# One ring of twelve tiles in place of two rings of six for a selective scan

## The chip, the cores and the metric

The kernel runs on one core of one Trainium2 chip, as one program. The metric is the device time of that program in microseconds (us); lower is better. For a profiled execution the span from the first to the last instruction on the core is given too.

## What is computed

The reference is a network of four layers on four images of 96 channels and 64x64 pixels. Layer 0 is the one that the change touches. It normalises the image, projects each pixel to 192 inner channels, convolves, and then runs a selective scan over the 4,096 pixels in four directions k. In each direction there are 16 states for each of the 192 channels:

```python
def step(h, inp):
    d_t, u_t, b_t, c_t = inp
    dA = jnp.exp(d_t[..., None] * A)
    h = dA * h + (d_t * u_t)[..., None] * b_t[:, :, None, :]
    y = jnp.einsum('bkdn,bkn->bkd', h, c_t)
    return (h, y)
```

So a decay dA and an inflow are made for every pixel, channel and state, the recurrence h = dA * h + inflow runs along the pixels, and the sum over the states of h times c gives the output y. Layer 1 is a deformable convolution (with gathers), layer 2 a Fourier mixer and a quantised feed-forward block, layer 3 a linear attention and another such block.

## The kernel before

**Units.** The scan of layer 0 is cut into units of 128 rows (8 channels x 16 states) by 1,024 pixels (T). There are 4 images x 4 directions x 4 stretches of pixels x 24 groups of 8 channels = 1,536 units. `Layer0.scan` (L898) goes through them in a written-out order and issues, for iteration n, pieces of several units at once, each on its own engine:

- `fetch` of unit n+5 (L964): a DMA on ACT's queue (L993) spreads 8 rows of the step sizes `de` over 128 rows of a tile `da` (512 KB).
- `decay` of unit n+2 (L1011): ACT turns `da` into exp(da * A), in place (L1014).
- `inflow` of unit n+1 (L1016): two matmuls on PE (L1020) spread 8 rows of `du` over 128 rows of a PSUM tile `db`; there are two such tiles.
- `enter` of unit n+1 (L1029): DVE multiplies `db` by the B rows of the tile `bc`, in place (L1034).
- `recur` of unit n (L1036): DVE's scan instruction reads `da` and `db` and writes the states `hh` (L1042).
- `weigh` of unit n-2 (L1046): POOL copies the last state (L1049) and multiplies `hh` by the C rows of `bc`, in place (L1051).
- `total` of the pair n-5 and n-4, in odd iterations (L1053): PE sums the states with eight matmuls that read `hh` (L1070). The text calls this the fold. For the first pair of a block it starts with matmuls on the tile `ad` (L1065).
- `settle` and `store` (L1078, L1083): ACT copies eight units' sums out of PSUM (L1081), and SP writes them to memory.

**Rings.** The tile pool gives the tiles of one name in turn: `da` has six buffers (L991) and `hh` six (L1040), each of 4 KB per partition. An instruction that starts to fill a buffer waits for all users of the tile that had it before. So the fetch of unit n+5, six units behind, waits until the scan of unit n-1 has read its `da`; and the scan of unit n waits until the fold of unit n-6 has read its `hh`.

**Order of the work.** The order on each engine is fixed when the program is built; every engine works through its list in that order. `layers23` (L1859) interleaves the scan with two streams of side work (the preparation of later images, layers 1 to 3 of earlier images). A planner (`Clock`, L206) holds an expected end for each engine; a stream may add a step if the engines that the step needs are not too far ahead of the planner's time (`has_room`, L231). `recur` adds 2.33 us to DVE's expected end, not before the decay and the fold that frees its buffer are expected to be done (L1039; the fold's time is passed in at L949). No wait on the chip comes from the planner: only the order does.

Of the kernel before, what the change touches and what calls it, by code (L numbers as in the profile page):

```python
# [8 lines left out]
F32 = mybir.dt.float32  # L9
# [14 lines left out]
T = 1024  # L24
# [335 lines left out]
class Net:  # L360
# [29 lines left out]
    def load(self, name, pool, tag=None):  # L390
        src = self.ins[name]
        t = pool.tile(list(src.shape), F32, name="w_" + name, tag=tag or "w_" + name)
        self.nc.sync.dma_start(t, src)
        return t
# [160 lines left out]
class Layer0:  # L555
# [342 lines left out]
    def scan(self):  # L898


        units = [
            Unit(b, k, step, g, i, q)
            for b in range(B)
            for k in ((1, 3, 0, 2) if b else (0, 1, 3, 2))
            for step in range(NT)
            for g in range(NG)
            for i in range(4)
            for q in range(2)
        ]
        ahead = 5  # L910
        loaded = 0
        clock = self.net.clock

        def at(m):
            return units[m] if 0 <= m < len(units) else None

        def made(u):
            return all(
                (u.b, u.k, both, 2 * u.j + h) in self.ready for both in (False, True) for h in range(2)
            )  # L920

        for n in range(len(units) + 7):
            for m in range(loaded, min(n + ahead + 1, len(units))):
                while not made(units[m]):
                    yield False
            if n == 0:
                while loaded < ahead:
                    self.fetch(units[loaded], units[loaded - 1] if loaded else None)
                    loaded += 1
                self.decay(at(0))  # L930
                self.decay(at(1))
                self.inflow(at(0))
                self.next = at(0)
                self.enter()

            for period, tick, load in ((24, 12, self.fetch_step), (8, 2, self.fetch_block)):
                u = at(n - n % period + period)
                if n % period == tick and u is not None and made(u):
                    load(u)
            for stage, m in ((self.inflow, n + 1), (self.decay, n + 2)):  # L940
                if at(m) is not None:
                    stage(at(m))
            if n % 2 == 1 and at(n - 5) is not None:
                self.total(at(n - 5), at(n - 4))
            if loaded < len(units):
                self.fetch(units[loaded], units[loaded - 1])
                loaded += 1
            if at(n) is not None:
                self.recur(at(n), at(n - 6).summed if n >= 6 else 0.0)  # L949
            if at(n - 2) is not None:  # L950
                self.weigh(at(n - 2))
            if n % 2 == 0 and at(n - 6) is not None and at(n - 6).i == 3:
                self.settle(at(n - 6))
            if n % 2 == 1 and at(n - 7) is not None and at(n - 7).i == 3:
                self.store(at(n - 7))
            clock.unit(self.scanned[1])
            self.next = at(n + 1)
            if self.next is not None:
                clock.enter, clock.entered = self.enter, self.next.spread
            yield True  # L960
            if clock.enter:
                self.enter()

    def fetch(self, u, before):  # L964


        sp, nc = self.sp, self.net.nc
        b, k, j, g, ts = u.b, u.k, u.j, u.g, u.ts
        c0 = 64 * g
        halves = [slice(j * T + h * CH, j * T + (h + 1) * CH) for h in range(2)]  # L970
        if not u.first_of_step:
            u.bc = before.bc
        elif u.bc is None:
            self.fetch_step(u)
        if u.first_of_step and u.step == 0:
            u.state = sp.tile([128, DI // D8], F32, name=f"st{u.key}", tag="st")
        else:
            u.state = before.state
        if not u.first_of_block:
            u.du, u.sums = before.du, before.sums  # L980
        else:
            u.sums = {"add": None}
            if u.du is None:
                self.fetch_block(u)
        if u.i == 1 and u.s == 1 and (k == 0 or u.back):
            add = u.sums["add"] = sp.tile([128, CH], F32, name=f"ad{u.key}", tag="ad", bufs=1)
            src = self.y_d[b][k - 2] if u.back else self.u_d[b]
            for h in range(2):
                nc.scalar.dma_start(add[64 * h : 64 * h + 64], src[c0 : c0 + 64, halves[h]])
        self.net.clock.add(ACT, 0.6, self.scanned[1])  # L990
        u.da = sp.tile([128, T], F32, name=f"da{u.key}", tag="da", bufs=6)  # L991
        src = self.de_d[b][k][c0 + 32 * u.q + u.i : c0 + 32 * u.q + 32 : 4, ts]
        nc.scalar.dma_start(u.da, src.unsqueeze(0).to_broadcast([NS, D8, T]))  # L993

# [41 lines left out]
    def recur(self, u, free):  # L1036

        nc, clock = self.net.nc, self.net.clock
        self.scanned = (self.scanned[1], clock.add(DVE, 2.33, max(u.decayed, free)))  # L1039
        u.hh = self.sp.tile([128, T], F32, name=f"hh{u.key}", tag="hh", bufs=6)  # L1040
        first = 0.0 if u.step == 0 else u.state[:, u.n : u.n + 1]
        nc.vector.tensor_tensor_scan(  # L1042
            u.along(u.hh), u.along(u.da), u.along(u.db), first, ALU.mult, ALU.add
        )
# [896 lines left out]
```

## Time and profile before

| | us |
|---|---|
| median of three runs | 8518.56 |
| the three runs, lowest to highest | 8506.89 to 8540.53 |
| profiled execution | 8585.65 |
| its span | 8582.9 |
| first scan starts, last scan starts | 183.3, 7487.1 |

The profile page gives the busy time of each engine over the span, and groups of instructions by line; "idle before, releaser" is the time for which the engine stood before instructions of that group, and the work of another engine (or DMA) that ended most of it. PE is the matmul engine and PEld its weight loads, DVE the vector engine, ACT the scalar engine, POOL the GpSimd; ACTq marks what ACT's sequencer issues itself, DMAs among it. The views of waits list who waited for whom, with the total in us, the number of times and the longest one.

### The profile page before, as it was taken

What the parts mean: (1) busy time and instruction counts of PE and PEld (TensorE: products, weight loads), DVE (VectorE), ACT (ScalarE), POOL (GpSimd) and SP (SyncE); (2) the same over time, 40 slices, a digit from 0 to 9 for tenths busy, and PEclk for the clock granted to TensorE, in tenths of its full rate; (3) what the DMA queues carried; (4) which work ended last, traced back from release to release, by engine and by line L of the source; (5) the groups of instructions that cost most, each with busy time, mean ns of one, the idle gap of its engine ahead of it and who ended that gap; (6) DMA issues with size and microseconds to landing.
All of it is one profiled execution on the core that took longest, in us unless ns stands there. A gap on an engine that the chain in (4) does not pass through costs nothing.

```text
span 8582.9 us, 96776 instructions
## 1 busy us (share of the span) xinstructions
PE 6491.0 (76%) x31814; PEld 2822.5 (33%) x31848; DVE 6815.3 (79%) x5122; ACT 4923.9 (57%) x8979; POOL 5616.1 (65%) x4308
## 2 busy tenths in 40 slices
PE   6775877679767668777767889777788777887487
PEld 2211221122222223311223555214454332464274
DVE  2799889888799888688898888888888887727614
ACT  5664566546567767755566667554667774423124
POOL 1565567656579888666688887675788986517600
PEclk9766877679668779877777888778788877888698
DMA  3677678868789888876788989777898886734410
GB/s 97 168 198 193 167 196 221 212 159 204 189 215 249 224 228 222 202 190 187 205 229 225 235 227 228 172 174 188 223 243 219 210 212 168 176 103 131 131 56 20
DMA packets 773929, 1608.29 MB, mean 187 GB/s; under 512 B 264081, under 2 KB 355757, under 8 KB 771222
## 3 DMA queue, kind: packets, MB, share of 16 engines
q10 hardware_dynamic: 244224, 843.17, 38.4%
q1 hardware_dynamic: 455478, 532.37, 24.0%
q0 software_dynamic: 73728, 226.57, 9.9%
q8 instruction: 255, 4.18, 0.2%
q14 instruction: 244, 2.00, 0.1%
HBM read 1345.43 MB, written 256.29 MB: 187 GB/s over the span
## 4 chain that ended last, share of the span: by engine, by line
PE 35%; DVE 30%; DMA 9%; issue 9%; ACT 9%; POOL 4%; SPq 1%; ACTq 1%; another core or an unknown queue 1%; DVEq 0%; POOLq 0%
DVE hh L1042 15%; DVE db L1034 8%; PE pc L763 4%; PE py L1070 4%; PE ps L1416 3%; PE f L1510 3%; POOL hh L1051 3%; ACT g L1395 2%; PE pd L1432 2%; PE db L1020 2%; DMA da<-de 2%; ACT da L1014 2%; PE h L1551 1%; PE zp L1576 1%; DMA m<-in_dft 1%
## 5 line engine op out<-in xcount | busy, mean ns | idle before, releaser
L1051 POOL TENSOR_TENSOR hh<-hh,bc 128x1024 f32<-128x1024 f32 x1536 | 3670.2, 2391 | 348.3 <-DVE hh L1042 230.6
L1042 DVE TENSOR_TENSOR_SCAN hh<-da,st,db 128x1024 f32<-128x1024 f32 x1152 | 2701.3, 2345 | 205.3 <-PE py L1070 68.5
L1034 DVE TENSOR_TENSOR db<-db,bc 128x1024 f32<-128x1024 f32 x1536 | 1863.1, 1213 | 561.7 <-PE db L1020 542.2
L1014 ACT ACTIVATE da<-da,w_al 128x1024 f32<-128x1024 f32 x1536 | 1736.9, 1145 | 496.0 <-DMA da<-de 144.5
L1383 POOL DMA_INDIRECT g<-table,idx x1152 | 1190.6, 1034 | 410.9 <-issue 185.9
L1020 PE MATMUL db<-du,rep 24*128 24x512 bf16 x3072 | 697.7, 453 | 802.4 <-DVE hh L1042 752.2
L1070 PE MATMUL py<-hh,w_fold 128*32 128x512 f32 x6144 | 1115.9, 786 | 30.9 <-POOL hh L1051 18.0
L1395 ACT ACTIVATE g<-g,wt 128x96 f32<-128x96 f32 x3456 | 965.0, 364 | 133.5 <-PE py L1070 38.9
L1042 DVE TENSOR_TENSOR_SCAN hh<-da,db 128x1024 f32<-128x1024 f32 x384 | 877.1, 2284 | 73.9 <-PE py L1070 23.6
L1416 PE MATMUL ps<-w_ident,g 128*96 128x128 f32 x3744 | 690.5, 331 | 246.3 <-issue 122.2
L1020 PEld LDWEIGHTS <-rep 24*128 24x128 bf16 x3072 | 160.3, 93 | 1914.3 <-issue 1278.0
L851 POOL TENSOR_TENSOR lw<-lw,w 128x512 f32<-128x512 f32 x192 | 244.1, 1272 | 710.9 <-DVE w L849 668.5
L1416 PEld LDWEIGHTS ps<-w_ident,g 128*96 128x96 f32 x3744 | 501.6, 149 | 594.1 <-issue 211.2
L1049 POOL COPY st<-hh 128x1 f32<-128x1 f32 x1152 | 234.6, 204 | 648.4 <-DVE hh L1042 612.7
L763 PE MATMUL pc<-pad,wc 96*128 96x512 f32 x1152 | 570.8, 632 | 8.8 <-ACT st L1424 2.6
L1424 ACT COPY st<-ps 96x384 f32<-96x384 f32 x384 | 180.3, 472 | 578.9 <-PE ps L1416 421.5
L882 PE MATMUL pr<-ex,w_ident 128*128 128x512 f32 x384 | 299.7, 872 | 146.7 <-DVE ex L872 57.1
L840 PE MATMUL pd<-xd,w_dtw 103*64 103x512 f32 (+1 forms) x512 | 281.5, 818 | 71.2 <-DVE rl L853 26.9
L1432 PE MATMUL pd<-st,wdc 96*128 96x256 f32 x1152 | 323.0, 434 | 11.6 <-ACT st L1424 4.2
L763 PEld LDWEIGHTS pc<-pad,wc 96*128 96x128 f32 x1152 | 217.2, 199 | 311.8 <-issue 291.0
L1519 ACT COPY d<-f 128x512 f32<-128x512 f32 x192 | 111.3, 582 | 315.2 <-PE f L1510 282.3
L1070 PEld LDWEIGHTS py<-hh,w_fold 128*32 128x32 f32 x6144 | 160.9, 125 | 385.9 <-issue 293.3
(259 smaller groups left out, 8798.4 us busy)
## 6 DMA issues: line engine op xcount, KB each, us to landing
da<-de ACTq DMA_DIRECT2D x1536, 512.0 KB
du<-du SPq DMA_DIRECT2D x1536, 96.0 KB
bc<-bcd SPq DMA_DIRECT2D x128, 512.0 KB
y<-yb SPq DMA_DIRECT2D x384, 128.0 KB
de<-rl SPq DMA_DIRECT2D x128, 256.0 KB
m<-in_dft SPq DMA_DIRECT2D x128, 256.0 KB
ad<-y ACTq DMA_DIRECT2D x192, 128.0 KB
table<-pix SPq DMA_DIRECT2D x256, 96.0 KB
```

The costliest lines, as they stand in the source:

```text
L763: nc.tensor.matmul(pp, lhsT=wc[:, q, g * 128 : (g + 1) * 128], rhs=pad[:, r0 + dy : r0 + dy + NR, dx : dx + W], start=(q == 0), stop=(q == 8),
L882: nc.tensor.matmul(pr, lhsT=net.ident, rhs=ex, start=True, stop=False)
L1014: self.net.nc.scalar.activation(u.da, u.da, AF.Exp, scale=self.al[:, a : a + 1])
L1020: self.net.nc.tensor.matmul(db[:, h, :], lhsT=self.rep[64 * u.q + 32 * h : 64 * u.q + 32 * h + 24], rhs=u.du[64 * u.q + 32 * h : 64 * u.q ...
L1034: self.net.nc.vector.tensor_mul(u.db, u.db, u.bc[:, 0, :])
L1042: nc.vector.tensor_tensor_scan(u.along(u.hh), u.along(u.da), u.along(u.db), first, ALU.mult, ALU.add)
L1051: self.net.nc.gpsimd.tensor_mul(u.hh, u.hh, u.bc[:, 1, :])
L1070: nc.tensor.matmul(py[p0 : p0 + 32], lhsT=self.fold[:, u.i, :], rhs=hc[:, h * CH : (h + 1) * CH], start=u.sums["add"] is None and u.i == 0 ...
L1383: nc.gpsimd.indirect_dma_start(out=g[:, k, :], out_offset=None, in_=self.tables[b % 2], in_offset=bass.IndirectOffsetOnAxis(ap=idx[:, n : ...
L1395: nc.scalar.activation(pixel, pixel, AF.Identity, scale=wt[:, n, c : c + 1])
L1416: nc.tensor.matmul(pt[:, k, :], lhsT=g[:, k, c * C : (c + 1) * C], rhs=net.ident, is_transpose=True, start=(c == 0), stop=(c == corners - 1),)
L1432: nc.tensor.matmul(po, lhsT=wdc[:, k, :], rhs=st[:, k, :], start=(k == 0), stop=(k == 8))
```

## The change

The scan writes its states into the tile that holds the decay, so `hh` is `da`. The ring of `hh` is gone, and the ring of `da` gets its six buffers too. The planner's entry for the scan takes the fold of unit n-9 in place of that of unit n-6.

```diff
@@ def scan(self):
             if at(n) is not None:
-                self.recur(at(n), at(n - 6).summed if n >= 6 else 0.0)
+                self.recur(at(n), at(n - 9).summed if n >= 9 else 0.0)
@@ def fetch(self, u, before):
         self.net.clock.add(ACT, 0.6, self.scanned[1])
-        u.da = sp.tile([128, T], F32, name=f"da{u.key}", tag="da", bufs=6)
+        u.da = sp.tile([128, T], F32, name=f"da{u.key}", tag="da", bufs=12)
         src = self.de_d[b][k][c0 + 32 * u.q + u.i : c0 + 32 * u.q + 32 : 4, ts]
         nc.scalar.dma_start(u.da, src.unsqueeze(0).to_broadcast([NS, D8, T]))
@@ def recur(self, u, free):
         self.scanned = (self.scanned[1], clock.add(DVE, 2.33, max(u.decayed, free)))
-        u.hh = self.sp.tile([128, T], F32, name=f"hh{u.key}", tag="hh", bufs=6)
+        u.hh = u.da
```

With twelve buffers in one ring, the fetch of unit n+5 now gets the buffer of unit n-7, whose last user is the fold of unit n-7.

## The prediction

> **What bounds the kernel now.** I first read the busy times of the page and the busy times by stretch, to see which stage sets the time. From 183 to 7490 us the scan runs; after it 1,093 us of side work are left, which the change doesn't touch. In the listing of instructions per engine, built from both kernels, the number behind the last scan is the same on DVE (765) and POOL (314) and nearly so on PE (3,284 before, 3,256 after) and ACT (596, 595). So the scan's stretch decides.
>
> ```profile
> core 0: us, PE busy (x) PEld busy (x) DVE busy (x) ACT busy (x) POOL busy (x), PEclk, DMA share, GB/s
> 183.00:7490.00 7307.00, 5561.07 (x25901) 2230.07 (x25934) 6273.50 (x4298) 4523.06 (x8263) 5246.10 (x3981) 0.78 0.80 205
> ```
>
> DVE is busy for 6273.5 of 7307 us (86%); 1,033 us of it are idle, and they are the most that any change of waits can win. The rows of groups say what a unit costs.
>
> ```profile
> L1051 POOL TENSOR_TENSOR hh<-hh,bc 128x1024 f32<-128x1024 f32 x1536 | 3670.2, 2391 | 348.3 <-DVE hh L1042 230.6
> L1042 DVE TENSOR_TENSOR_SCAN hh<-da,st,db 128x1024 f32<-128x1024 f32 x1152 | 2701.3, 2345 | 205.3 <-PE py L1070 68.5
> L1034 DVE TENSOR_TENSOR db<-db,bc 128x1024 f32<-128x1024 f32 x1536 | 1863.1, 1213 | 561.7 <-PE db L1020 542.2
> L1014 ACT ACTIVATE da<-da,w_al 128x1024 f32<-128x1024 f32 x1536 | 1736.9, 1145 | 496.0 <-DMA da<-de 144.5
> ```
>
> Then the views of waits. The reader is to see that DVE's largest wait is for the inflow (PE db), which the change doesn't touch; that the scan waits for the fold 89 times; and that ACT too waits for the scan.
>
> ```profile
> DVE db L1034 <- PE db L1020: 542.2, 234, 25.1
> ACT da L1014 <- DMA da<-de: 144.5, 80, 6.4
> ACT da L1014 <- DVE hh L1042: 105.7, 30, 15.0
> DVE hh L1042 <- PE py L1070: 92.1, 89, 5.3
> DVE hh L1042 <- ACT da L1014: 33.7, 18, 4.4
> ACT g L1395 <- DVE hh L1042: 29.6, 15, 3.4
> ACT yb L1081 <- DVE hh L1042: 12.3, 7, 2.5
> ```
>
> A decay, a scaling of gathered rows or a copy of sums on ACT reads nothing that the scan writes. These waits are those of the fetch (L993) that stands ahead in ACT's list. A piece of the timeline shows one wait for the fold, 1.84 us ahead of the scan at 5016.41:
>
> ```profile
> 5013.34 1.23 DVE L1034 TENSOR_TENSOR db<-db,bc 128x1024 f32<-128x1024 f32 x1
> 5014.94 1.26 PE L1070 MATMUL py<-hh,w_fold 128*32 128x512 f32 x8
> 5016.13 0.39 PE L1020 MATMUL db<-du,rep 24*128 24x512 bf16 x2
> 5016.41 2.35 DVE L1042 TENSOR_TENSOR_SCAN hh<-da,st,db 128x1024 f32<-128x1024 f32 x1 [1.84 <-PE py L1070]
> 5018.67 1.21 DVE L1034 TENSOR_TENSOR db<-db,bc 128x1024 f32<-128x1024 f32 x1
> ```
>
> Without the wait the scan could start near 5014.6 and end near 5016.9; the next inflow is there at 5016.5, so DVE would go on at once. This wait is on the path locally.
>
> [...] work that needs no scan stood behind a fetch that did (105.7 us for decays alone). [...]
>
> **The change part by part.**
>
> *In-place write.* No row shows an in-place scan. The nearest pair is on DVE: L849 writes w over w (median 682 ns for 128x512), L853 writes rl from other tiles (680 ns). From both sides: +2 ns per 512 columns is +4 ns on a scan, 6 us over 1,536; a gain is excluded, as nothing less is computed. I take 0 and keep +6.
>
> *The scan's wait for the fold goes.* In the listing 746 scans wait for PE before and none after; 89 of the waits cost time, 92.1 us. That is the ceiling. Pairing each such scan in the trace with the inflow of the next unit, the inflow had landed about 2.0 us (median) before DVE's next multiply; cutting each wait to this slack leaves 60 us that shift the next multiply too. Some of it is given back when DVE meets its next wait for an inflow. I take three quarters, 45 us; ends 0 and 92. Late next is the inflow itself: it stands on PE behind the same fold.
>
> *The fetch's wait moves from the scan of n-1 to the fold of n-7.* Of 1,536 fetches 1,380 wait for DVE before; after, 267 do, 1,231 wait for POOL and 110 for PE. In the trace 116 fetches stand on ACT until the scan ends, 252 us of ACT's idle time. Behind a held fetch stand on ACT: the next decays, the sums' copy (L1081), for which PE's next block of folds waits, and side work. Most of these holds are in stretches where DVE runs without a gap (scans 3.61 us apart, at 2413.52 and 2417.13): there ACT waits for DVE, and freeing ACT wins nothing. What DVE can get back is bounded by 105.7 + 29.6 + 12.3 = 147.6 us of the waits above; DVE itself waited for decays for only 33.7 us. I take 15% of the 147.6, 23 us; ends 0 and a third, 49 us.
>
> *The new wait.* The fold of n-7 ended, in the trace, 2.8 us at the earliest and 9.9 us in the median before the fetch of n+5 was issued. So at the present spacing it never binds: 0 us. Its cover is that spacing. If DVE runs further ahead of POOL, ACT stops at L993, with decay n+3 and side work behind it. That is the slower rival below.
>
> *DMAs.* Same number, size and place in ACT's list; SP's and POOL's lists hold the same instructions. Some fetches go out about 2 us earlier, which can only help the decays that waited for them. 0 us.
>
> *The order.* The planner now thinks the scan free sooner, so fewer side steps are let in early. In the two listings a side instruction moves by 0 units in the median and mostly by under 9; the ends of the lists are equal. I take 0, within +-20 us.
>
> Sum: 0 - 45 - 23 + 0 = -68 us, against the profiled execution 8585.65 - 68 = 8518. That execution is 67 us (0.8%) above the median of the runs shown, so I carry the difference over: 8518.56 - 68 = 8450 us.
>
> **The rivals.**
>
> *Given back at the inflow (8505).* DVE's 542.2 us for the inflow say that PE's list is what is late; a scan that starts sooner then waits longer for the next inflow. For it: the inflow stands behind the fold. Against it: the 2.0 us of slack. Then about 14 us remain of the 68.
>
> *All of it counts (8377).* 92 + 49 = 141 us. For it: in the chain of work that ended last, steps from the fold to the scan and from DVE to the fetch on ACT both occur, some tens each. Against it: chains nearly as long run through ACT's scalings and PE's sums (L1395, L1416).
>
> *ACT stops at the new wait (8575).* With no ring of its own the scan may run ahead until the fetch stops ACT. It decides where POOL can't keep up: from 6000 to 7000 us POOL is busy 854.85 us for 231 units, 3.70 us each, above the 3.61 of a scan at full pace. If the 330 or so units from 6000 to 7490 each hold ACT for 0.5 us and a third reaches DVE, that is 55 us: 8574. Against it: units there come every 4.3 us (1000/231), so POOL has room.
>
> *The change doesn't do what it says*: excluded, the listing shows 0 waits of scans for PE.
>
> **How the numbers follow.** Forecast 8450 with chance 0.45 (own range 8415 to 8480); all of it 0.15; given back 0.27; ACT stops 0.13. About 0.5% (43 us) is what a measurement of this kernel tells from no change: under 8476 is faster, over 8561 slower. Faster: nearly all of the first, all of the second, a little of the third: 0.58. Slower: 0.12. Same: 0.30. The range from 8380 to 8560 reaches over the forecast and the given-back case; it leaves out the further half of "all of it" and most of "ACT stops".
>
> **What would show it.** Right: no wait of the scan for PE py (92.1 to 0); the waits of ACT's decays, scalings and copies for DVE's scan (147.6) falling to near 0; the scan still at 2,345 ns; DVE's wait for the inflow growing by less than 50 us; last scan near 7,420 us in place of 7,487. Given back: the inflow's wait near 630 us. ACT stops: ACT's work waiting for PE's fold or for POOL's L1051 by over 100 us. The prediction is wrong if the scan's duration changes, or if the wait for the inflow falls or grows by 100 us or more, since then the order and not the buffers decides.

## The result and the profile after

The changed kernel takes 8462.06 us in the median of four runs (8455.38 to 8470.7), the kernel before 8529.55 us in the median of its four (8506.89 to 8546.57). The two medians are 67 us apart. The ratio of the runs is 0.9906, with a 95% interval from 0.9884 to 0.9928: about 0.9% faster, which is some 80 us. The forecast was 8450 us, 68 us faster. The number came out; the experiments below show that the reasons for it mostly did not.

The stretch of the scan on the page of the changed kernel's profile, then the groups of the scan and of its neighbours:

```profile
core 0: us, PE busy (x) PEld busy (x) DVE busy (x) ACT busy (x) POOL busy (x), PEclk, DMA share, GB/s
184.00:7419.00 7235.00, 5512.39 (x25928) 2191.97 (x25927) 6277.89 (x4297) 4515.50 (x8264) 5235.20 (x3981) 0.78 0.81 207
```

```profile
L1051 POOL TENSOR_TENSOR da<-da,bc 128x1024 f32<-128x1024 f32 x1536 | 3664.1, 2387 | 351.6 <-DVE da L1042 233.3
L1042 DVE TENSOR_TENSOR_SCAN da<-da,st,db 128x1024 f32<-128x1024 f32 x1152 | 2701.1, 2345 | 124.1 <-ACT da L1014 12.8
L1034 DVE TENSOR_TENSOR db<-db,bc 128x1024 f32<-128x1024 f32 x1536 | 1865.4, 1214 | 614.7 <-PE db L1020 613.1
```

The stretch is 72 us shorter (7,235 in place of 7,307 us) at the same busy time of DVE (6278 and 6274 us). The in-place scan takes the same 2345 ns. The idle time ahead of the scan has fallen, that ahead of the multiply of the inflow has grown. The profiled spans as wholes lie 129 us apart (8582.9 and 8453.6 us), which overstates the change: 58 us of it lie behind the start of the last scan (1,096 us before, 1,037 after). The kernel with the buffers alone, which has the lists of before on every engine, takes 1,048 us there; this points to the spread of single executions.

The views of waits of the changed kernel (who waited for whom, total us, times, longest):

```profile
DVE db L1034 <- PE db L1020: 613.1, 311, 25.1
ACT da L1014 <- DMA da<-de: 166.9, 92, 11.0
ACT da L1014 <- PE py L1070: 60.4, 14, 11.7
ACT yb L1081 <- PE py L1070: 53.8, 14, 13.0
ACT da L1014 <- POOL da L1051: 40.7, 9, 8.4
DVE da L1042 <- ACT da L1014: 32.4, 17, 11.4
ACT g L1395 <- POOL da L1051: 17.5, 4, 6.7
```

The scan's wait for the fold (92.1 us) is gone, and so are the waits of decays, scalings and copies for the scan (147.6 us). But DVE's wait for the inflow stands at 613.1 us, 71 us more than the 542.2 of before. Some new waits stand on ACT, for POOL's weighing (40.7 + 17.5 us, 13 times). In all 13 a fetch lies on ACT between the instruction that waits and the busy one before it, as in all 52 waits of decays, scalings and copies for the scan (147.6 us) in the trace of before; this fits work that is held up behind a fetch in ACT's list. Taken alone, this page would almost pass for the forecast come true, but three quarters of the scan's wait have come back at the inflow. What it can't tell is that two things changed at once: the buffers, and the order of the side work.

### The profile page after: what moved, and what is told of

Its sections match the earlier page's. It is cut to its first block, busy times and chain, and to the rows that moved or that the text cites. A ratio compares the mean times of both kernels' runs of the same rounds, so it can differ in the third digit from the quotient of the medians.

```text
span 8453.6 us, 96209 instructions
## 1 busy us (share of the span) xinstructions
PE 6424.4 (76%) x31848; PEld 2772.6 (33%) x31848; DVE 6826.4 (81%) x5122; ACT 4914.8 (58%) x8979; POOL 5621.2 (66%) x4308
## 4 chain that ended last, share of the span: by engine, by line
PE 32%; DVE 26%; DMA 12%; POOL 11%; issue 9%; ACT 8%; SPq 2%; ACTq 1%; DVEq 0%; POOLq 0%
DVE da L1042 12%; POOL da L1051 7%; DVE db L1034 7%; PE pc L763 3%; DMA da<-de 3%; PE py L1070 3%; PE ps L1416 3%; PE f L1510 3%; POOL g L1383 3%; PE pd L1432 2%; PE db L1020 2%; ACT g L1395 2%; ACT da L1014 2%; DMA du<-du 1%; PE h L1551 1%
## 5 line engine op out<-in xcount | busy, mean ns | idle before, releaser
L1051 POOL TENSOR_TENSOR da<-da,bc 128x1024 f32<-128x1024 f32 x1536 | 3664.1, 2387 | 351.6 <-DVE da L1042 233.3
L1042 DVE TENSOR_TENSOR_SCAN da<-da,st,db 128x1024 f32<-128x1024 f32 x1152 | 2701.1, 2345 | 124.1 <-ACT da L1014 12.8
L1034 DVE TENSOR_TENSOR db<-db,bc 128x1024 f32<-128x1024 f32 x1536 | 1865.4, 1214 | 614.7 <-PE db L1020 613.1
L1383 POOL DMA_INDIRECT g<-table,idx x1152 | 1206.8, 1048 | 360.2 <-issue 178.7
L1070 PE MATMUL py<-da,w_fold 128*32 128x512 f32 x6144 | 1091.8, 784 | 43.6 <-issue 25.2
L1042 DVE TENSOR_TENSOR_SCAN da<-da,db 128x1024 f32<-128x1024 f32 x384 | 877.0, 2284 | 54.7 <-ACT da L1014 19.6
L1416 PEld LDWEIGHTS ps<-w_ident,g 128*96 128x96 f32 x3744 | 483.5, 144 | 601.3 <-issue 178.9
L1049 POOL COPY st<-da 128x1 f32<-128x1 f32 x1152 | 232.2, 202 | 674.1 <-DVE da L1042 655.8
L1070 PEld LDWEIGHTS py<-da,w_fold 128*32 128x32 f32 x6144 | 158.1, 124 | 381.1 <-issue 300.3
L1432 PEld LDWEIGHTS pd<-st,wdc 96*128 96x128 f32 x1152 | 243.2, 219 | 104.2 <-issue 39.5
```

The source lines that it names most:

```text
L1034: self.net.nc.vector.tensor_mul(u.db, u.db, u.bc[:, 0, :])
L1042: nc.vector.tensor_tensor_scan(u.along(u.hh), u.along(u.da), u.along(u.db), first, ALU.mult, ALU.add)
L1051: self.net.nc.gpsimd.tensor_mul(u.hh, u.hh, u.bc[:, 1, :])
L1070: nc.tensor.matmul(py[p0 : p0 + 32], lhsT=self.fold[:, u.i, :], rhs=hc[:, h * CH : (h + 1) * CH], start=u.sums["add"] is None and u.i == 0 ...
L1383: nc.gpsimd.indirect_dma_start(out=g[:, k, :], out_offset=None, in_=self.tables[b % 2], in_offset=bass.IndirectOffsetOnAxis(ap=idx[:, n : ...
L1416: nc.tensor.matmul(pt[:, k, :], lhsT=g[:, k, c * C : (c + 1) * C], rhs=net.ident, is_transpose=True, start=(c == 0), stop=(c == corners - 1),)
```

## The experiments

Every ratio is to the kernel before, run beside it. "Buffers" is the part of the change that acts on the chip (the ring of twelve, the states in place); "order" is what the planner's entry for the fold does to the lists of instructions.

### The two parts of the change, each alone

Buffers alone: the changed kernel with the planner's old entry; every engine's list is as in the kernel before.

```diff
-                self.recur(at(n), at(n - 9).summed if n >= 9 else 0.0)
+                self.recur(at(n), at(n - 6).summed if n >= 6 else 0.0)
```

> The change without its planner part: in-place states in one ring of twelve, the instruction order of the kernel before. Theory 'buffers' (both waits that the ring of six made were worth about 68 us together): 60 to 80 us faster than before, ratio 0.991. Rival 'order' (the new order of the side work makes the gain): within 20 us of before, ratio 0.998 to 1.002. The scan waits 0 us for the fold under either.

Measured: 0.999 (0.9976 to 1.0004), no gain clear of noise. Order alone: the kernel before with the planner's new entry (the same line the other way round), two rings of six.

> The planner's part of the change alone: two rings of six, the instruction order of the changed kernel. 'Buffers': within 20 us of before, ratio 0.998 to 1.002, and about 90 us of waits of the scan for the fold. 'Order': 60 to 80 us faster, ratio 0.991.

Measured: 0.9928 (0.9903 to 0.9952), 61 us faster. My theory falls: the order, which I had put at 0, makes most of the gain, and the buffers, which I had put at 68 us, make little. (Part of the gain of order alone goes with a higher clock; see the last section.) DVE's waits show where the buffers' gain went. In each fence the scan's wait for the fold, where there is one, stands with the wait for the inflow. Buffers alone:

```profile
DVE db L1034 <- PE db L1020: 640.5, 291, 25.2
```

Order alone:

```profile
DVE db L1034 <- PE db L1020: 539.6, 292, 22.8
...
DVE hh L1042 <- PE py L1070: 95.6, 76, 9.0
```

With the order of before, the two waits of the old rings come to 542.2 + 92.1 = 634.3 us, and the ring of twelve leaves 640.5: by this count all is given back at the inflow. With the new order it is 539.6 + 95.6 = 635.2 against 613.1: 22 us are kept. The account that fits: the inflow stands on PE behind the same folds and side work as before, so a scan that starts sooner is followed by a longer wait for it.

The same can be asked of DVE itself: ahead of which of its instructions does it stand idle between the first scan and the last (us, one execution of each kernel, from the traces)?

| | ahead of scans | ahead of the inflow's multiply | ahead of side work |
|---|---|---|---|
| before | 279 | 537 | 218 |
| buffers alone | 173 | 617 | 247 |
| order alone | 290 | 518 | 182 |
| both (the changed kernel) | 179 | 590 | 189 |

The buffers alone take 106 us from the scans; 80 come back at the multiply and 29 at the side work, so nothing is left. The order alone takes 36 us from the side work and 19 from the multiply.

### Each of the two waits alone, in the new order

The ring of twelve, in which one of the old waits is put back as a dependency between the same instructions. No work is added, but a wait for one engine more can take a semaphore instruction of its own: 396 more on ACT's queue in the first kernel, 502 more on DVE's in the second. On DVE such instructions cost nothing that shows: the kernel before has 1,910 of them at the scans and the changed kernel 1,320, and the gaps of under 0.2 us ahead of scans come to 137 and 143 us in all. The order of the work on all engines is that of the changed kernel. In the first the fetch waits again for the scan of n-1 (of the 1,536 fetches 1,390 then wait for DVE):

```diff
-        nc.scalar.dma_start(u.da, src.unsqueeze(0).to_broadcast([NS, D8, T]))
+        ins = nc.scalar.dma_start(u.da, src.unsqueeze(0).to_broadcast([NS, D8, T]))
+        if old is not None:
+            self.after(ins, old.scan)
```

Here `self.after(a, b)` makes a wait for the end of b, and `old` is unit n-1 (in the second edit unit n-6).

> The changed kernel, in which each fetch is made to wait again for the scan of unit n-1 (an added dependency, no instruction more); the scan stays free of the fold. My sum gives the scan's wait 45 us and the fetch's 23 us: so 45 us faster than before, ratio 0.9947, and some 150 us of ACT's work behind fetches that wait for the scan. Rival 'the fetch's wait was the larger part': under 25 us faster, ratio over 0.997.

Measured: 0.9892 (0.9868 to 0.9917). In the second the scan waits again for the fold of n-6 (748 scans wait for PE):

```diff
+        if old is not None:
+            self.after(u.scan, old.fold)
```

> The changed kernel, in which each scan is made to wait again for the fold of unit n-6 (an added dependency, no instruction more); the fetch stays free. My sum: 23 us faster than before, ratio 0.9973, with about 90 us of waits of the scan for the fold. Rival 'the fetch's wait was the larger part': 45 us or more faster, ratio 0.995 or lower. If the two parts overlap rather than add, both this and the other single part lose more than half of the whole.

Measured: 0.9942 (0.9921 to 0.9963). My two expectations were reckoned from an order worth nothing, so neither theory's figures could fit; what counts is the four ratios of one order. With 0.9928 for both waits and 0.9906 for none, freeing the scan is worth 0.36% (31 us) whether the fetch waits or not. Freeing the fetch is worth nothing: 0.14% slower in both pairs. Each such difference of two ratios carries about +-0.33% (the root of the two intervals' halves, squared and added), so the first is just clear of zero and the second is not. For the first there is more: the runs with both waits (8475.91 to 8502.49 us) and those with the fetch's alone (8440.32 to 8468.92) do not overlap. In this order, fetches held by the scan cost no time that can be measured; my 23 us were wrong. The waits in these two runs, the fetch held and then the scan held:

```profile
DVE db L1041 <- PE db L1027: 627.4, 327, 26.2
```

```profile
DVE db L1039 <- PE db L1025: 523.5, 292, 23.6
...
DVE da L1047 <- PE py L1077: 96.2, 79, 8.5
```

(The added lines shift the line numbers: L1041 and L1039 are the multiply, L1047 the scan.) Again 96.2 us of the scan's waits turn into some 100 us more at the inflow. By this sum nothing would be kept, while the times say 31 us. The profiled execution with the scan held is the fastest of its eight runs (8461.12 us, their median 8501.75), so these two lines can't show what the times do.

### Is the new order better by rule or by luck?

The planner's own clock, as it stands while the program is built, shows what the entry does there. With the fold of n-6 it lets the scan wait for a fold 333 times, for 283.5 us in all; the chip had 89 waits and 92.1 us. With n-9 it never waits (nor with n-7 or n-8, whose order is the same). When a scan is entered, the planner's DVE stands 7.0 us ahead of its pace in the median with n-6, and 1.9 us with n-9. Since side work may be added when an engine is not too far ahead of DVE's end, a DVE that seems late lets PE's side work in early, ahead of inflows. So a rule is possible: a planner without the wait spaces the side work better. The rival is luck: any other order would have moved the time too. To tell them apart I made other orders under the same rule, by a nudge to the planner's cost of a scan that changes nothing else:

```diff
-        self.scanned = (self.scanned[1], clock.add(DVE, 2.33, max(u.decayed, free)))
+        self.scanned = (self.scanned[1], clock.add(DVE, 2.34, max(u.decayed, free)))
```

All have the ring of twelve. With the fold of n-6, 2.34 and 2.30 us:

> The ring of twelve with the planner waiting for the fold of n-6 (as in the run without the planner part), and the scan's cost in the planner nudged from 2.33 to 2.34 us: another order of the side work, the same planner rule, the same waits on the chip. Theory 'rule' (the order is worse because the planner believes in a wait of 283 us that the chip does not have, and so lets side work in too early): within 20 us of before, ratio 0.997 to 1.003. Rival 'luck' (any new order shifts the time by some tens of us either way): a ratio that may lie anywhere from 0.988 to 1.008, at 0.992 or lower as easily as near 1.

Measured: 0.9988 (0.9975 to 1.0001).

> As the other nudge of the rule with n-6, with 2.30 us in place of 2.33. 'Rule': ratio 0.997 to 1.003. 'Luck': scattered, as likely 0.992 as 1.

Measured: 0.9982 (0.9963 to 1.0001). With the fold of n-9, 2.34, 2.30 and 2.36 us:

> The changed kernel (the planner's wait for the fold of n-9, which never binds in the planner) with the scan's cost nudged from 2.33 to 2.34 us: another order, the same rule as the changed kernel. 'Rule': 55 to 90 us faster than before, ratio 0.9895 to 0.9935. 'Luck': scattered, as likely near 1 as near 0.991.

Measured: 0.998 (0.9963 to 0.9996).

> The changed kernel's rule (the fold never binds in the planner), with the scan's cost in the planner at 2.30 us in place of 2.33. The first nudge of this rule, to 2.34, lost the gain (0.998). 'Luck of one order': 0.996 to 1.003, as the four other orders. Rival 'the rule is better on the whole, the first nudge fell out badly': 0.989 to 0.994.

Measured: 0.9999 (0.9982 to 1.0016).

> As the nudge down, with 2.36 us. 'Luck of one order': 0.996 to 1.003. 'The rule is better on the whole': 0.989 to 0.994. One of the two nudges near 0.991 and the other near 1 would leave an advantage of the rule of a few tenths of a per cent open.

Measured: 0.9943 (0.9925 to 0.9962). Four orders of the new rule thus give 0.9906, 0.9943, 0.998 and 0.9999; three of the old give 0.9982, 0.9988 and 0.999. The rule doesn't bring the gain: two of its four orders have 0.2% or nothing. Luck of the order is the better account, and whether the rule has an advantage of a few tenths of a per cent on the average stays open with four against three.

### How much does side work cost that is let in too early?

The changed kernel, with a greater and a smaller lead in the planner:

```diff
-AHEAD = (3.0, 3.0, 5.0, 7.0)
+AHEAD = (8.0, 8.0, 10.0, 12.0)
```

> The changed kernel, in which the planner may let each engine run 5 us further ahead of its time (AHEAD 8, 8, 10, 12 in place of 3, 3, 5, 7). With the fold of n-6 the planner's DVE stands 7.0 us ahead of the pace in the median, with n-9 1.9 us: some 5 us. 'Rule, through side work that is let in too early': the gain of the changed kernel is mostly lost, ratio 0.996 to 1.004, and DVE's wait for the inflow grows by 30 us or more over the changed kernel's 613. Rival 'the lead is harmless': ratio 0.989 to 0.993.

Measured: 1.0761 (1.073 to 1.0792), 7.6% slower; far beyond what I had expected. Its wait for the inflow:

```profile
DVE db L1034 <- PE db L1020: 1330.1, 370, 30.6
```

The 717 us more at the inflow are close to the whole loss, about 730 us over the changed kernel. So side work that is let in too early is a real cost; here it is shown with a lever large enough to see. The lever acts on all four engines at once. That it is PE's share of it which costs is read from this wait, and not tried alone.

> The changed kernel with the planner's engines let 1 us less far ahead (AHEAD 2, 2, 4, 6). 5 us further ahead cost 7.6%. If the cost of side work that is let in too early goes on below today's lead, a fifth of it or less is won: ratio to before 0.98 to 0.99, with DVE's wait for the inflow under 560 us. If today's lead is at its best, side work is late instead: ratio 0.995 to 1.01.

Measured, with 2, 2, 4 and 6: 0.9994 (0.9977 to 1.0012). Less lead is no better; it is again one more order, and not a clean step on a curve.

### A third pair for the buffers

The order of the last nudge (2.36, fold of n-9) with the two rings of six:

```diff
-        u.hh = u.da
+        u.hh = self.sp.tile([128, T], F32, name=f"hh{u.key}", tag="hh", bufs=6)
```

and six buffers for `da`.

> The order of nudge9_far (0.9943) with the two rings of six of the kernel before: a third pair, in which only the buffers and their waits differ. If the buffers are worth what the first two pairs showed (0.1 to 0.2% of the time, most of the scan's wait given back at the inflow): ratio to before 0.9945 to 0.997, with the scan's wait for the fold and DVE's wait for the inflow together within 25 us of what nudge9_far shows for the inflow alone. If my sum of 68 us were right for the buffers: ratio 1.001 to 1.003.

Measured: 0.9957 (0.9943 to 0.9971), against 0.9943 with the ring of twelve. Two rings of six, then the ring of twelve in the same order:

```profile
DVE db L1034 <- PE db L1020: 516.9, 246, 26.7
DVE hh L1042 <- PE py L1070: 88.1, 82, 5.5
```

```profile
DVE db L1034 <- PE db L1020: 614.3, 287, 25.6
```

605.0 us with the scan's wait, 614.3 without: nothing kept by this count. In three orders the buffers are worth 0.10, 0.22 and 0.14% (9 to 19 us of 8,530), none of them clear of zero alone, all of one sign.

## Why the prediction was right in its number and wrong in its reasons

That the number came out is luck: the order, put at 0, gave about what the two terms of the buffers were to give and mostly did not.

- **In-place write: right.** 0 us. The 1,152 scans that read a column of `st` take 2345 ns in the mean before and after, the other 384 take 2284 ns before and after. POOL's weighing beside them takes 2391 and 2387 ns.
- **The scan's wait for the fold: right that it goes, wrong in what is kept.** The step that failed is "I take three quarters, 45 us". The waits for the fold and for the inflow together came to 634.3 us with the rings of six and 640.5 with the ring of twelve in the same order; in the other two orders 22 us were kept and 9 lost. The rival "given back at the inflow" was the true account of the buffers; its 14 us fit the 9 to 19 measured. (In the new order the scan's freedom alone gave 31 us; with the fetch's wait moved as well, 19 are left.) I had read the slack of 2.0 us between an inflow's landing and the next multiply as a gain that lasts. It is a shift of one multiply. PE's list does not get shorter by it, and DVE stands again at a later inflow or at side work: of the 106 us taken from the scans by the buffers alone, 80 and 29 us came back there. The 89 gaps ahead of the scan (92.1 us) did come from a ring with too few tiles: the same twelve tiles in one ring removed them all. But the time went into the next gap, whose cause was not the buffers.
- **The fetch's wait: wrong.** 23 us expected (15% of 147.6 is 22), 0 or a small loss measured in the new order (0.14% slower in two pairs; the old order was not tried). This fits the prediction's own remark that most holds lie where ACT is ahead of DVE and waits for a scan in progress.
- **The new wait: wrong that it never binds.** The spacing of the old trace (2.8 us at least) was made by the old rings themselves: the fetch of n+5 waited for the scan of n-1, and that scan for the fold of n-7, so a whole scan (2.3 us) always lay between. A cover that the change takes away is no cover. In the changed kernel the longest recorded wait ahead of a fetch is 7.8 us:

```profile
L993 ACTq EVENT_SEMAPHORE  x1053: 17/17/7767, 255.5 to 7389.7; - x176
```

  (Before, the same records last 17 ns each; there the wait for the scan shows as ACT's idle time ahead of the fetch.) Decays and scalings wait 58.2 us for POOL's weighing, and with the copies 129.2 us (60.4 + 53.8 + 15.0) for the fold. Such waits for the fold came to 105.9 us before. The sign that the prediction set for "ACT stops", over 100 us of such waits, was there before the change and could not tell. No run takes the new wait away alone. Where it replaced the fetch's old one (order alone against the scan held), the time was 0.14% longer, not clear of zero: that rival found its wait, and its 55 us did not come.
- **The order: the term that was mis-sized, from 0 to about -61 us.** "I take 0, within +-20 us" rested on a median move of 0 units and on equal ends of the lists. Neither says how much an order is worth: nudges of the same kind moved the time by up to 0.9%. By the starts of the scans, in one execution each, the second half of the units (768 to 1535), in which layers 1 to 3 of the first images run beside the scan, takes 3,561 us before, 3,567 with the buffers alone, 3,509 with the order alone and 3,495 after. The first half takes 3,742, 3,747, 3,746 and 3,737. So in these executions most of the gain lies in the second half. DVE's idle time in the whole stretch is 1,034 us before, 1,036 with the buffers alone, 990 with the order alone and 957 after. The order's share stands ahead of DVE's side work more than ahead of the multiply (36 and 19 us). The eight orders with the ring of twelve (the one with the greater lead left aside) agree, in one execution each: DVE stands 189 and 208 us ahead of side work in the two that are clearly faster (0.9906 and 0.9943), 232 to 275 us in the six that are within 0.2% of before; ahead of the multiply it is about 590 us in the two and 587 to 657 in the six. Which placements save it was not settled; the idle time is spread over many waits of a few us.
- **What was to show it.** The scan's wait, ACT's waits and the last scan (7,416 us, 7,420 forecast) came as forecast, but the inflow's wait grew by 71 us where I had allowed 50, and at 613 us it lay near the 630 set for "given back". That was the sign that the buffers' gain had been given back, and that something else had paid. The last scan's time proved nothing: two unlike causes give it.

## What to carry to other kernels

When a program's order comes from a planner, a change to a buffer and to the planner's model of it are two changes; try each alone, with the lists of instructions held fixed for the first, before either is credited. A wait taken off an engine that then waits for another's queue can be given back there (here 634.3 us of DVE's two waits became 640.5 us of one): add up all of that engine's waits in both versions, and count only what the sum loses. One execution gives this to some tens of us only (the profiled one of the kernel before lay 56 us above the median of its four runs), so let the times of many runs decide. And before a rule for an order is believed, nudge it: if a nudge of 0.01 us in a cost loses the gain (here 0.998 in place of 0.9906), one good order was found and not a better rule.

## What I had not expected of the chip

Repeated runs of one program spread by about 1% (8485.88 to 8575.47 us in 28 runs of the kernel before), and the time goes with the granted TensorE clock of the run: within the kernels with 14 runs or more, 0.001 of clock less goes with about 4.6 us more (correlations from -0.5 to -0.8). Which of the two is the cause isn't shown. It doesn't explain the gain of the change: carried to one clock of 0.789 by that slope, the changed kernel's runs come to 8468 us and those of the kernel before to between 8527 and 8559 in its four sets of runs. But it goes with part of the gain of order alone. That kernel's six runs have a mean clock of 0.7918, the 28 of the kernel before beside them 0.7861; at one clock, about 28 of the 54 us between the two means are left. If the new order itself brings the higher clock, all of it is the order's; that is not shown. A high clock is not enough: the old rule with 2.30 us has 0.7902, as high as the changed kernel's 0.7903, and no gain. Nor is it needed: the new rule with 2.36 us is 0.6% faster at 0.7872. The profiled execution before (8585.65 us) lay above all runs shown with it; a ratio over several runs was needed.
